# Two graph layers with nested Strassen-Winograd products: products in six steps, an order of its own for the first, second and last pair, and first transfers in a fixed order

## The chip, the cores and the metric

The kernel runs on one core of a Trainium2 chip. Its engines are TensorE (PE; PEld in the profile is its weight load), VectorE (DVE), ScalarE (ACT), GpSimd (POOL) and SyncE (SP), which here issues all DMA transfers. The metric is the time of one execution on the device in microseconds, lower being better. Products are accumulated in PSUM, which has eight banks of 512 fp32 columns per partition[...].

## The reference, cut to what matters

There are 64 graphs of 256 nodes with 512 features, all fp32. Two layers follow each other, each with a residual and a layer norm.

```python
def _L0_gnn_ref(x, adj, W):
    deg = jnp.sum(adj, axis=-1, keepdims=True)
    agg = jnp.einsum('bij,bjf->bif', adj, x) / jnp.maximum(deg, EPS)
    cat = jnp.concatenate([x, agg], axis=2)
    return jax.nn.relu(jnp.einsum('bnf,of->bno', cat, W))

def _L1_gnn_ref(X, adj, mask, Wqk, Wv):
    q, k = jnp.split(X @ Wqk, 2, axis=-1)
    v = X @ Wv
    agg = jnp.einsum('bij,bjd->bid', adj, k * mask[:, :, None])
    w = inv_scale * mask * jnp.einsum('bid,bid->bi', q, agg)
    return jax.nn.softmax(w, axis=1)[:, :, None] * v

x = _layernorm(x + _L0_gnn_ref(x, adj, L0_gnn_W), axis=-1)
x = _layernorm(x + _L1_gnn_ref(x, adj, nodemask, L1_gnn_Wqk, L1_gnn_Wv), axis=-1)
```

`x` is 64 x 256 x 512, `adj` 64 x 256 x 256, `W` 512 x 1024, `Wqk` 512 x 1024 and `Wv` 512 x 512.

## The kernel before

**Tiling.** Two graphs make a pair, so there are NP = 32 pairs. Nodes lie in two tiles of 128 (NT), features in four (NF). In layer 1 the two weight halves of Wqk are multiplied once, at the start, into one 512 x 512 matrix (`weight_product`, 16 matmuls of 512 columns from the tile `shared`), so that q·(adj k) becomes (x M)·(adj x).

**Products.** Each 512 x 512 by 512 product for a pair is cut by the Strassen-Winograd scheme into seven block products P1 to P7. Those named in `INNER` (P1, P2, P5, P3, P4) are cut a second time by the same scheme (`inner`): seven 256-column matmuls each, some into a scratch bank `w`, from which VectorE or ScalarE carry each partial result into the product's two banks `q`. The others (`outer`) are four plain 512-column matmuls. The sums of operand blocks are made by GpSimd (`inner_sums`, `fourth_sums`, `adj_sums`) and VectorE (`outer_sums`, `sums_T`). The adjacency product (`gather`) is one level of the same scheme.

**Units.** `inner` returns four closures: `first`, `second`, `third` and `last`, where `third` holds two matmuls and `last` two. `layer0` and `layer1` bind letters to the lists of closures: i, k, m, p, q, r, s are P1, P5, P2, P6, P7, P3, P4 of layer 0; J, N, K, H, Q, L, P are P1, P5, P2, P6, P7, P3, P4 of layer 1; a to g and A to G are the seven parts of the two gathers. `pw`, `pu`, `py` and `pf` are the four pairs of banks; the scratch bank of each product is passed by the caller.

**Order.** Nothing is issued directly. VectorE, ScalarE and GpSimd operations go through a `Recorder`, matmuls through `mm` and transfers through `send`, all into a `Plan`, with the bytes that they touch and an assumed duration. The string `ORDER` says in what sequence the letters' closures are called within a loop pass over pairs; the pass for pair j does layer 0 of pair j and layer 1 of pair j - 1. `when(...)` hangs further work on counts of letters done. TensorE's recorded sequence gives every step a due time; `Plan.order` then lists all engines' instructions, choosing by due time among the steps that its assumed durations say can start soon (within `SLACK`). The list so made is the program order of each engine, which runs its queue strictly in that order. After the loop the last pair's layer 1 is written out with `run(...)` calls.

**Lines that the steps below speak of.** L270 is the recorder's one line, so all VectorE, ScalarE and GpSimd work carries it; rows are told apart by their tiles. L355 is `mm`, L361 the transpose by TensorE, L790 the transpose of the last scores, L371 is `send`. Tiles: `own` is a pair's rows (result of layer 0, then x1, then the output); `xT`, `x1T` are the transposed inputs of the two layers, `_s` and `_i` their outer and inner sums; `t`, `t_i` are weight sums; `tv` the sums for the gathers; `fifth` a kept partial result; `less`, `var`, `rstd`, `shift` the columns of a layer norm (`norm_parts`): `less` is minus the mean, made by VectorE from `sum`; `row`, `top`, `total` and `probs` belong to `softmax`. There the scores of a pair, 128 x 4, are put into a 128 x 32 tile `wide`, turned, stored to `dram` and read back into all partitions as `row`, whose maximum `top` VectorE takes over 512 columns.

**Start.** Ten matmuls on a tile of ones come first. Transfers are sent in recorded order as far as due times allow; the built order begins with two `w` blocks, two `wqk` blocks, `xT`, two `wqk` blocks and two `w` blocks. `weight_sums` makes the sums of W0 and W1 on VectorE.

Of the kernel before, what the change touches and what calls it, by code (L numbers as in the profile page):

```python
# [16 lines left out]
P = 128  # L17
Q = 32
# [7 lines left out]
INNER = ("P1", "P2", "P5", "P3", "P4")  # L26
SLOTS_X = {"P1": 0, "P2": 1, "P5": 2, "P3": 2, "P6": 0, "P7": 1, "P4": 0}
SLOTS_X1 = {"P1": 0, "P2": 1, "P5": 2, "P6": 0, "P7": 1, **({"P3": 2, "P4": 0} if "P7" in INNER else {"P3": 0, "P4": 1})}
ORDER = ("L k k i i i L k k i m p p m p p q m q q q s r m s r r r a s b s d e J J c J J f K g K K K N H H "
         "N Q A D H H Q Q C E Q N G N P P B P P F L L")  # L30
# [32 lines left out]
class Plan:  # L63
# [78 lines left out]
    def latest(self):  # L142

        before, left, open_, n = defaultdict(list), {}, [], 0
        for s in self.steps:
            left[s] = len(s.next)
            for t, fresh in s.next:
                before[t].append((s, fresh))
# [72 lines left out]
def vec_cost(op, out, ins, more):  # L221
# [6 lines left out]
    if op in ("scalar_tensor_tensor", "tensor_scalar"):  # L228
        if n < 16:
            return 0.08, 0.158, both  # L230
        by_column = len(ins) > len(wide)
        return (n / 960 + (0.133 if by_column else 0.078),
                n / 960 + (0.21 if by_column else 0.15) + (0.08 if more else 0), both)
# [72 lines left out]
def resnorm_kernel(  # L306
# [58 lines left out]
    def send(out, in_):  # L365
        o, i = ap_of(out), ap_of(in_)
        n = columns_of(o) * o.ap[0][1] * 4
        issue, sent, done = (0.66, 0.66, 3.0) if n == 64 * 1024 else (0.41, n / 300000, 3.0)
        if i.ap[0][0] == 0:
            sent = 3.5  # L370
        plan.record("SP", lambda: nc.sync.dma_start(out, in_), [o], [i], issue, done, sent=sent)  # L371
# [32 lines left out]
    def load_xT(j, home=home_x):  # L404
        Xs[j] = Side(home, *sums_x, 0, SLOTS_X)
        for k in range(2):
            send(Xs[j].a[:, k].rearrange("p h e t n -> p (h e) (t n)"),
                 x_t[2 * j + k].rearrange("(c p) n -> p c n", p=P))
# [3 lines left out]
    for a in range(NA):  # L412
        send(wqk.rearrange("p (h a) f -> a p h f", h=2)[a],
             wqk_t.rearrange("(h a p) f -> a p h f", p=P, h=2)[a])
    w0_of = w_t.rearrange("(k h p) o -> k p h o", p=P, h=H)
    for k in (0, 2):
        send(w0[:, k * H:(k + 1) * H, :], w0_of[k])
    load_xT(0)
    for k in (3, 1):
        send(w0[:, k * H:(k + 1) * H, :], w0_of[k])  # L420
# [16 lines left out]
    drams = [dram.tile([P, Q], F32, name=f"dram{k}") for k in (0, 1)]  # L437
# [5 lines left out]
    def weight_sums(w, name):  # L443
        b11, b21, b12, b22 = (w[:, k * H:(k + 1) * H, :] for k in range(4))
        t1, t2, t4 = (mem.tile([P, H, F], F32, name=f"{name}{k}") for k in (1, 2, 4))
        it = mem.tile([P, 3, len(INNER), HF], F32, name=f"{name}i")
# [3 lines left out]
        def inner_of(p, b):  # L450
            if p not in INNER:
                return
            n = INNER.index(p)
            c11, c12, c21, c22 = (b[:, e, h * HF:(h + 1) * HF] for e in range(2) for h in range(2))
            i1, i2, i4 = (it[:, r, n] for r in range(3))
# [67 lines left out]
    def inner(p, X, sides, w, q, done=lambda: None, onto=None):  # L523
# [42 lines left out]
        def third():  # L566
# [5 lines left out]
            else:  # L572
                act.copy(q[1][:, :HF], lo)
                vec.tensor_add(q[1][:, HF:], lo, fifth[0])
            mm(q[0][:, :HF], X.chunk(block, 0, 1), b["B21"])

        def last():
            mm(q[1][:, :HF], X.chunk(block, 1, 1), b["T4"])
            mm(q[0][:, HF:], s(3), b["B22"])
            done()  # L580
        return [first, second, third, last]

    def product(p, X, sides, w, q, done, onto=None):
        if p in INNER:
# [88 lines left out]
    def norm_parts(src, total, n=NT):  # L673
        rstd, shift, less, var = (small(x, [P, n]) for x in ("rstd", "shift", "less", "var"))

        def squares():
            vec.tensor_scalar(less, total, -1.0 / F, None, op0=OP.mult)
# [70 lines left out]
    def softmax(j):  # L748
        w = wide[j % 2]
        scale_scores(j, w[:, :2 * NT].rearrange("p (k t) -> p k t", k=2))  # L750
        turned = small("turned", [P, Q], 2)
        vec.transpose(turned, w)
        d = drams[j % 2]
        send(d, turned)
        row = ring("row", [P, P // Q, 2 * NT * Q])
# [3 lines left out]
        rk = row.rearrange("p a (k c) -> p k a c", k=2)  # L759
        p = small("probs", [P, 2, NT], 2)  # L760
        vec.reduce_max(top, rk, axis=AX.XY, negate=True)
# [41 lines left out]
    def layer0(j, X, o, u, y):  # L803

        own, yt = owns[j], ys[j]
        make = lambda p, w, q, done, onto=None: product(p, X, W0, w, q, done, onto)
        return {
            "i": make("P1", pw[0], u, lambda k: act.copy(own[:, k, 0], u[k])),
            "k": make("P5", pw[1], y, lambda k: act.copy(yt[:, k, 1], y[k])),
            "m": make("P2", pw[0], o, lambda k: act.copy(own[:, k, 0], o[k]), own[:, :, 0]),  # L810
            "p": make("P6", pw[1], u, lambda k: vec.tensor_add(yt[:, k, 0], u[k], yt[:, k, 1])),
            "q": make("P7", pw[0], u, lambda k: vec.tensor_add(yt[:, k, 1], u[k], yt[:, k, 1])),
            "r": make("P3", pw[1], y, lambda k: act.copy(yt[:, k, 0], y[k]), yt[:, :, 0]),
            "s": make("P4", pw[0], u, lambda k: act.copy(own[:, k, 1], u[k])),
        }

    def layer1(j, Y, q, o, u, y, w1_, w2, w5, w3, w4, w6, w7):
# [3 lines left out]
        make = lambda p, w, q, done, onto=None: product(p, Y, W1, w, q, done, onto)  # L821
# [9 lines left out]
        def add_p5(k):  # L831
            vec.tensor_add(v[:, k], y[k][:, None, :].to_broadcast([P, NT, F]), v[:, k])
        return {
            "J": make("P1", w1_, u, lambda k: act.copy(q[:, k], u[k])),
            "K": make("P2", w2, o, lambda k: act.copy(q[:, k], o[k]), q),
            "H": make("P6", w6, u, lambda k: act.copy(v[:, k, 0], u[k])),
            "Q": make("P7", w7, u, lambda k: act.copy(v[:, k, 1], u[k])),
            "N": make("P5", w5, y, add_p5),
            "P": make("P4", w4, u, lambda k: dot(u[k], k, 1)),
            "L": make("P3", w3, y, lambda k: act.copy(v[:, k, 0], y[k]), v[:, :, 0]),  # L840
        }, dots

    def run(order, **units):
        for name in order.split():
            units[name].pop(0)()

# [14 lines left out]
    W0 = weight_sums(w0, "t0_")  # L861
# [6 lines left out]
    W1 = weight_sums(w1, "t1_")  # L868
# [5 lines left out]
    for j in range(NP):  # L874
# [4 lines left out]
        units, made = layer0(j, X, o, u, y), Counter()  # L879
        waiting = []  # L880

        def when(done, work):
            waiting.append((Counter(done), work))

        def start_gather0():
            units.update(gather("abcdefg", sumsA.pop(j), sums_T(ys[j]), pw[1], y[1], y[0],
                                own=own, rdeg=rdegs.pop(j)))

        def end_gather0():
            place = norm0(j)  # L890
            mask_adj(j)
            if place:
                when("PPPPL" if j else "", place)

        def x_sums(*ps):
            for p in ps:
                if p in INNER:
# [21 lines left out]
        when("kkkk", lambda: (fourth_sums(X), x_sums("P3")))  # L919
        when("iiii", lambda: x_sums("P6"))  # L920
        when("mmmm", lambda: x_sums("P7"))
        when("pppp" if "P6" in INNER else "iiii", lambda: x_sums("P4"))
        when("ppppqqqqrrrr", start_gather0)
        when("rrrrssss", next_x)
# [3 lines left out]
        else:  # L928
# [4 lines left out]
            new, dots = layer1(j - 1, Y, q_at, o2, u2, y2, pw[0], y[0], pw[1], pw[1], pw[0], pw[0], pw[1])  # L933
            made["L"] = 4 - len(ahead)
# [3 lines left out]
            def y_sums(*ps):  # L938
                for p in ps:
                    if p in INNER:  # L940
# [14 lines left out]
            def start_gather1():  # L955
                units.update(gather("ABCDEFG", sumsM.pop(j - 1), sums_T(owns[j - 1]), pw[0], o2[1], o2[0],
                                    aggs[j - 1]))
            when("LLLL" if j > 1 else "mmmm", start_layer1)
            when("JJJJ", lambda: y_sums("P6"))
            when("KKKK", lambda: y_sums("P7" if "P7" in INNER else "P4"))  # L960
            when("HHHH", lambda: (fourth_sums(Y), y_sums("P4" if "P7" in INNER else "P3")))
            if "P7" in INNER:
                when("HHHHNNNN", lambda: y_sums("P3"))
            when("gKKKK", start_gather1)
            when("BFKKKK", dots)
            when("ABCDEFG", next_adj)
        for name in ORDER.split():
            if name.isupper() and j == 0 or name == "L" and j == 1 and not made["J"]:
                continue
            units[name].pop(0)()  # L970
            made[name] += 1
# [109 lines left out]
```

## Time and profile before

| What | Value |
|---|---|
| Time, median of 3 runs | 1866.63 us (1865.25 to 1867.9) |
| Span of the profiled execution | 1865.2 us, 26366 instructions |
| TensorE clock granted, mean | 0.995 |
| One pair in the middle of the loop (two of 56.7 us, from 435.6) | PE 56.45, PEld 42.6, DVE 49.1, ACT 38.7, POOL 30.8 us busy |
| Front, 0 to 50 us | PE 45.95, DVE 34.7, POOL 24.0 us busy |
| 50 to 100 us | PE 46.6, DVE 45.8, ACT 28.4, POOL 36.1 us busy |
| 1800 us to the end | PE 48.6, DVE 46.3, ACT 43.2, POOL 17.6 us busy |
| `less<-sum`, VectorE, x126 | 138 ns shortest, 400 median, 722 longest; 50.6 us in all |
| `top<-row`, VectorE, x31 | 675 ns mean |

How to read it: a row of instructions gives start, duration, engine, line, operation, the tile written and those read, shapes, and how many in a row were merged ("x2"). The bracket at the end is the idle time of that engine before it and what ended the wait. An fp32 matmul is carried out in two passes, each with its own row, so "x2" is mostly one matmul of the program. The duration of a PE row is modelled and overlaps the next one; the distance of two starts is the real pace. An idle bracket counts from that modelled end, so it states less than what was lost against the pace.

### The profile page before, as it was taken

The page shows a single profiled execution, that of the slowest core. Times are in us where ns is not written, and L with a number is a line of the kernel's source. Part 1 is how long each engine was busy: PE and PEld are TensorE (multiplying, and loading weights), DVE is VectorE, ACT ScalarE, POOL GpSimd, SP SyncE. Part 2 cuts the span into 40 slices and gives each one's busy share as a digit, 9 for nine tenths or more (in the row PEclk, how much of TensorE's full clock was granted, in tenths as well). Part 3 has the DMA queues.
Part 4 walks back from the last instruction along what each step waited for, and adds up shares of the span by engine and source line. Part 5 has one row for each costly group of instructions (what it writes and reads, how often), then busy time and mean ns, then how long its engine had stood idle before and what let it go on. Part 6 is the DMA issues. An engine that isn't in the chain of part 4 may idle for free.

```text
span 1865.2 us, 26366 instructions
## 1 busy us (share of the span) xinstructions
PE 1834.0 (98%) x7382; PEld 1374.0 (74%) x7382; DVE 1595.6 (86%) x3511; ACT 1245.2 (67%) x3115; POOL 996.1 (53%) x1511
## 2 busy tenths in 40 slices
PE   9999999999999999999999999999999999999996
PEld 5777777777777777777777777777777777777774
DVE  6988988888888889888889888888888898888886
ACT  3656766667766668666667666677666686666665
POOL 4745555565545565545655555654456555456532
PEclk9999999999999999999999999999999999999998
DMA  7133333433333343233333333333333432343302
GB/s 238 46 78 99 101 82 97 109 107 95 103 87 96 97 116 93 81 103 108 97 102 99 84 97 108 108 94 98 91 98 97 115 92 79 106 109 97 98 11 74
DMA packets 380721, 181.35 MB, mean 97 GB/s; under 512 B 263712, under 2 KB 345248, under 8 KB 380576
## 3 DMA queue, kind: packets, MB, share of 16 engines
q1 hardware_dynamic: 380576, 179.67, 34.9%
q8 instruction: 60, 0.98, 0.2%
q14 instruction: 85, 0.70, 0.1%
HBM read 114.10 MB, written 34.06 MB: 79 GB/s over the span
## 4 chain that ended last, share of the span: by engine, by line
PE 83%; DVE 14%; issue 1%; ACT 1%; DMA 0%; SPq 0%; POOL 0%; ACTq 0%; DVEq 0%
PE bank L355 83%; DVE own L270 7%; DVE bank L270 3%; DVE less L270 1%; DVE y L270 1%; DVE x1T L270 1%; DMA shared<-wqk_t 0%; ACT junk L270 0%; DVE rdeg L270 0%; ACT own L270 0%; PE bank L361 0%; DVE turn L270 0%; DVE x L270 0%; DVE t_i L270 0%; ACT fifth L270 0%
## 5 line engine op out<-in xcount | busy, mean ns | idle before, releaser
L270 ACT COPY fifth<-bank 128x256 f32<-128x256 f32 x384 | 144.0, 376 | 302.0 <-PE bank L355 300.2
L270 POOL TENSOR_TENSOR x1T_i<-x1T 128x128 f32<-128x128 f32 (+1 forms) x128 | 81.0, 634 | 455.3 <-PE bank L355 315.8
L270 DVE TENSOR_TENSOR bank<-bank,fifth 128x256 f32<-128x256 f32 (+1 forms) x576 | 259.2, 456 | 44.1 <-PE bank L355 23.1
L270 ACT COPY shared<-bank 128x512 f32<-128x512 f32 x314 | 182.2, 582 | 66.1 <-PE bank L355 60.6
L355 PE MATMUL bank<-tv,sa 128*128 128x256 f32 x768 | 217.3, 379 | 0.2 <-DVE tv L270 0.2
L355 PE MATMUL bank<-w,x1T 128*128 128x512 f32 (+1 forms) x512 | 206.5, 486 | 0.0
L355 PEld LDWEIGHTS bank<-tv,sa 128*128 128x128 f32 x768 | 145.1, 190 | 81.9 <-issue 53.3
L270 ACT COPY bank<-bank 128x256 f32<-128x256 f32 (+1 forms) x352 | 145.4, 420 | 84.6 <-PE bank L355 74.2
L355 PE MATMUL bank<-w,xT 128*128 128x256 f32 (+1 forms) x496 | 200.0, 486 | 0.0
L270 ACT ACTIVATE junk<-own,less 128x512 bf16<-128x512 f32 x254 | 183.5, 723 | 21.0 <-DVE less L270 18.7
L270 DVE TENSOR_TENSOR y<-bank,y 128x512 f32<-128x512 f32 x192 | 132.2, 689 | 75.9 <-PE bank L355 72.1
L270 ACT ACTIVATE own<-own,shift,rstd 128x512 f32<-128x512 f32 x254 | 194.9, 824 | 2.8 <-DVE shift L270 2.6
L355 PE MATMUL bank<-t_i,x1T_i 128*128 128x256 f32 x640 | 187.3, 382 | 1.3 <-POOL x1T_i L270 0.7
L270 DVE TENSOR_TENSOR shared<-bank,shared 128x512 f32<-128x512 f32 (+1 forms) x157 | 137.6, 891 | 52.3 <-PE bank L355 52.0
L355 PE MATMUL bank<-t_i,xT_i 128*128 128x256 f32 x640 | 181.2, 379 | 0.0
L270 DVE SCALAR_TENSOR_TENSOR own<-bank,rdeg,own 128x256 f32<-128x256 f32 x384 | 174.8, 476 | 5.8 <-PE bank L355 1.9
L270 ACT COPY y<-bank 128x512 f32<-128x512 f32 x256 | 149.2, 585 | 45.1 <-PE bank L355 44.8
L355 PEld LDWEIGHTS bank<-t_i,xT_i 128*128 128x128 f32 x640 | 118.7, 190 | 72.0 <-issue 58.6
L355 PE MATMUL bank<-t,x1T_s 128*128 128x512 f32 (+1 forms) x384 | 168.2, 521 | 0.0
L355 PE MATMUL bank<-t,xT_s 128*128 128x512 f32 (+1 forms) x384 | 158.5, 521 | 0.1
L355 PEld LDWEIGHTS bank<-t_i,x1T_i 128*128 128x128 f32 x640 | 117.4, 189 | 28.1 <-issue 8.8
L270 ACT COPY own<-bank 128x512 f32<-128x512 f32 x192 | 112.5, 588 | 35.5 <-PE bank L355 35.1
(158 smaller groups left out, 4402.3 us busy)
## 6 DMA issues: line engine op xcount, KB each, us to landing
x<-x SPq DMA_DIRECT2D x64, 512.0 KB, 3.6
xT<-x_t SPq DMA_DIRECT2D x62, 512.0 KB, 3.8
out<-own SPq DMA_DIRECT2D x62, 512.0 KB, 3.8
x1T<-turn SPq DMA_DIRECT2D x480, 64.0 KB, 2.1
adj<-adj_t SPq DMA_DIRECT2D x64, 256.0 KB, 2.9
turn<-adj SPq DMA_DIRECT2D x64, 256.0 KB, 2.9
row<-dram SPq DMA_DIRECT2D x31, 256.0 KB, 5.3
w<-w_t SPq DMA_DIRECT2D x4, 512.0 KB, 7.4
```

The costliest lines, as they stand in the source:

```text
L270: self.plan.record(self.name, lambda: call(out, *args, **kwargs), outs, ins, busy, done, port)
L355: plan.record("PE", lambda: nc.tensor.matmul(ps, a, b, start=start, stop=True, skip_group_check=True), [ps], [a, b], busy, busy + 0.165, w ...
```

## The change

**Inner products in six steps.** `third` and `last` are split, so that each closure has one matmul (only `first` has two): first, second, third, fourth, last, closing. `INNER` becomes one tuple per layer, with the same members.

**Orders.** Four strings take the place of one string and the written-out `run` calls: `ORDER0` for pair 0, `ORDER1` for pair 1, `ORDER` for the others, and `ORDER9` for the last pair's layer 1, where `S` stands for scores, turns and exponentials and `Z` for the division. `when` takes the names of products (all their closures) instead of repeated letters.

**Scratch banks.** `HOME` and `HOME9` name for each letter one of the eight banks, counted through pu, py, pf, pw.

**First transfers.** `send` can take a due time; the nine first blocks get the fixed sequence wqk 0, w 0, w 2, wqk 1, xT, wqk 2, w 3, wqk 3, w 1.

**Work moved between engines.** W1's sums for P5, P3 and P4 go to GpSimd (12 operations of 256 columns); the weight sums `i` are three tiles instead of one. `less` is made by ScalarE. In `softmax`, VectorE takes the maximum of each of the 128 turned rows (32 columns) into a 33rd column before the store; `top` is then taken over 16 columns, and the exponential reads `row` without them.

**Planner.** No step is due later than 6 us after TensorE's recorded end, and `tensor_scalar` counts as using the port that VectorE shares with GpSimd.

```diff
+HOME = "i6 k7 m6 p5 q1 r7 s6 a7 b2 c3 J6 K2 H7 Q1 N7 L7 P6 A6 B4 C5"
+HOME9 = "J7 K7 H5 Q2 N6 L7 P1 A2 B3 C1"
-ORDER = ("L k k i i i L k k i m p p m p p q m q q q s r m s r r r a s b s d e J J c J J f K g K K K N H H "
-         "N Q A D H H Q Q C E Q N G N P P B P P F L L")
+ORDER0 = ("i k k i i i i k i k p k k p p p m r q r m m m q r q q s r r m s r s s a m b s s d e c f g")
+ORDER1 = ("k k i i i i i k k i m k p k p p p q m m r q m m q r q s s s m r r s r s r J a b s J J d J e J c "
+          "J f K H g K K K H Q K N K Q A H H N N D N C E Q Q N N G B L P P F P L L P P P")
+ORDER = ("i i i i k k k L k L L k i i p m m k m p q p q m p m r q m q s s s s r r s r J r a J J J b J d J "
+         "s e c J f K K g H K H K H K K N N H Q N A Q D Q C E Q N G P F B N N L L P P L P P P L")
+ORDER9 = ("A J J J D J C J J E K B H G H N Q N H K N N F K H Q N K Q Q N K K P P L P P L L P P S L L L Z")
...
+            s.due = min(s.due, self.clock + 6.0)
...
+    for n, (what, k) in enumerate(((load_wqk, 0), (load_w0, 0), (load_w0, 2), (load_wqk, 1), (first_xT, 0), (load_wqk, 2), (load_w0, 3), (load_wqk, 3), (load_w0, 1))):
+        what(k, n - 1000.0)
...
-        it = mem.tile([P, 3, len(INNER), HF], F32, name=f"{name}i")
+        it = [mem.tile([P, len(INNER[layer]), HF], F32, name=f"{name}i{r}") for r in (1, 2, 4)]
...
+            sub = gp.tensor_sub if p in by_gp else vec.tensor_sub
...
+
+        def fourth():
             mm(q[0][:, :HF], X.chunk(block, 0, 1), b["B21"])
 
         def last():
             mm(q[1][:, :HF], X.chunk(block, 1, 1), b["T4"])
+
+        def closing():
             mm(q[0][:, HF:], s(3), b["B22"])
             done()
-        return [first, second, third, last]
...
+        return [first, second, third, fourth, last, closing]
...
-            vec.tensor_scalar(less, total, -1.0 / F, None, op0=OP.mult)
+            act.activation(less, total, AF.Copy, scale=-1.0 / F)
...
-        turned = small("turned", [P, Q], 2)
-        vec.transpose(turned, w)
+        turned = small("turned", [P, Q + 1], 2)
+        vec.transpose(turned[:, :Q], w)
+        vec.reduce_max(turned[:, Q:], turned[:, :Q], axis=AX.X)
...
-        vec.reduce_max(top, rk, axis=AX.XY, negate=True)
+        vec.reduce_max(top, rk[:, :, :, :, Q], axis=AX.XY, negate=True)
+        rk = rk[:, :, :, :, :Q]
```

## The prediction

> **What bounds the kernel now.** I read the page first (busy shares, chain of waits), then the list of who waits for whom on PE, then the timeline in four places. Durations are of the profiled execution, span 1865.2 us; that run took 1867.0 us, and the runs shown go from 1865.25 to 1867.9.
>
> ```profile
> PE 1834.0 (98%) x7382; PEld 1374.0 (74%) x7382; DVE 1595.6 (86%) x3511; ACT 1245.2 (67%) x3115; POOL 996.1 (53%) x1511
> ...
> PE 83%; DVE 14%; issue 1%; ACT 1%; DMA 0%; SPq 0%; POOL 0%; ACTq 0%; DVEq 0%
> ...
> PE bank L355 <- DVE bank L270: 7.6, 30, 0.5
> PE bank L355 <- DMA shared<-wqk_t: 2.8, 1, 2.8
> ```
>
> TensorE is the bound and hardly idles; what it waits for repeatedly is VectorE writing into a PSUM bank, 30 times, once for each pair that uses ORDER. But a busy PE hides part of its loss, because the modelled end of a matmul runs past the start of the next. I therefore measure loss by starts. Each fp32 matmul appears as two passes; one of 256 columns takes 0.43 us from start to start (below, 603.31 to 603.74), one of 512 takes 0.86.
>
> ```profile
> 603.31 0.59 PE L355 MATMUL bank<-w,x1T_i 128*128 128x256 f32 x2
> ...
> 603.59 0.72 DVE L270 TENSOR_SCALAR less<-sum 128x2 f32<-128x2 f32 x1
> 603.74 0.59 PE L355 MATMUL bank<-tv,adj 128*128 128x256 f32 x2
> ...
> 604.23 0.47 DVE L270 SCALAR_TENSOR_TENSOR own<-bank,rdeg,own 128x256 f32<-128x256 f32 x1
> ...
> 604.61 0.59 PE L355 MATMUL bank<-own,adj 128*128 128x256 f32 x2
> 604.62 0.68 DVE L270 TENSOR_TENSOR bank<-bank,y 128x512 f32<-128x512 f32 x1
> ...
> 605.45 0.67 PE L355 MATMUL bank<-t_i,x1T 128*128 128x256 f32 x2 [0.25 <-DVE bank L270]
> ...
> 605.96 0.38 PE L355 MATMUL bank<-t_i,x1T_i 128*128 128x256 f32 x1
> ```
>
> This is the steady loss. From 604.61 to 605.45 are 0.84 us for 0.43 us of work, and from 605.45 to 605.96 another 0.08 too many: 0.49 us. A further 0.10 us occurs once per pair at a `t_i,xT_s` product (in the pass starts). A pair takes 56.7 us, so 0.59 us is 1%; 30 pairs make 17.7 us.
>
> ```profile
> 4.63 0.42 DVE L270 TENSOR_TENSOR t_i<-w 128x256 f32<-128x256 f32 x1 [3.54 <-DMA w<-w_t]
> 7.74 6.63 PE L355 MATMUL bank<-shared 128*128 128x512 f32 x11 [2.79 <-DMA shared<-wqk_t]
> 10.46 0.34 PEld L355 LDWEIGHTS bank<-shared 128*128 128x128 f32 x1 [0.52 <-issue]
> 11.20 0.19 PEld L355 LDWEIGHTS bank<-shared 128*128 128x128 f32 x1 [0.40 <-issue]
> ...
> 88.28 0.70 PE L355 MATMUL bank<-t_i,x1T_i 128*128 128x256 f32 x2 [0.61 <-DVE t_i L270]
> 89.56 1.13 PE L355 MATMUL bank<-tv,adj 128*128 128x256 f32 x4 [0.57 <-DVE tv L270]
> 92.45 1.13 PE L355 MATMUL bank<-own,adj 128*128 128x256 f32 x4 [0.86 <-ACT bank L270]
> 94.69 0.70 PE L355 MATMUL bank<-t_i,x1T_i 128*128 128x256 f32 x2 [0.68 <-POOL x1T_i L270]
> ...
> 1849.58 1.05 PE L355 MATMUL bank<-total,fifth 1*128 1x1 f32 x8 [0.68 <-DVE total L270]
> 1849.84 0.72 ACT L270 ACTIVATE junk<-own,less 128x512 bf16<-128x512 f32 x1 [0.28 <-DVE less L270]
> ```
>
> The front: the first transfer (a `w`) has landed at 4.63, the warm-up matmuls on `ones` end at 4.99, but the first real matmul starts at 7.74, and its passes then come 0.85 us apart instead of 0.43 until 11.2. Lost: 2.75 + 1.75 = 4.5 us. The first two pairs: starts against the pace give 0.8, 0.8, 1.1 and 0.8 us at the four places shown, and with the small ones between 15 and 200 us 7.5 us in all. The end: PE's last matmul is over at 1850.6; ScalarE then normalises the last but one pair's rows (begun at 1849.84) ahead of the last pair's, and 14.6 us pass to the end.
>
> **What the Trainium skill says.** "TensorE: Matmul & The Clock Gate", Part 1: TensorE runs at half clock until about 3.4 us of activity and falls back when idle. The trace agrees: the 512-column passes at 7.74 to 11.2 take double. "SBUF — State Buffer", section "SBUF: two separate sides": VectorE and GpSimd share a port pair, locked for a whole instruction. The trace agrees: `less`, 256 numbers, takes 0.14 us at the tail and 0.72 at 603.59, beside a GpSimd add of 0.73 us begun at 603.56. "Perfetto Trace Analysis", section "Optimization Strategy": the same gap repeating on the saturated engine can mean too little PSUM for the next tile. Here the repeated gap is indeed a PSUM bank's half, but VectorE's queue is what makes it late.
>
> **The change, part by part.** Both programs hold 3726 PE instructions of equal kinds and 876 on SP, so the work of the bound engine is unchanged; only losses can move.
>
> (1) The loop. The matmul that stalls (`t_i,x1T`, last unit of K) needs a 512-wide VectorE addition that follows K's third product (the `w,x1T_i` at 603.31). By the built programs' order three 256-column matmuls lay between the two: 1.29 us. In the changed program five do, one of 512 columns: 4 x 0.43 + 0.86 = 2.57 us. Before, the addition began 0.9 us after its product had drained (603.31 + 0.43 + about 0.17 = 603.9, to 604.62), because `less` held VectorE until 604.31. Now `less` goes to ScalarE, and VectorE's `top` over 512 columns (675 ns mean, once per pair) becomes a maximum over 32 columns before the store and one over 16 after it; I estimate these at 0.15 us each, from the small VectorE rows of 0.14 to 0.17. VectorE sheds 2 x 0.40 + 0.38 = 1.2 us of its 49 per pair. Against it: in the new VectorE queue five instructions stand between the preceding `bank<-bank,y` and this addition: 3 x 0.43 to 0.47 of `own<-bank`, a `tv` of 0.68, a 512-wide `own` of about 0.83, 2.9 us; with both additions 4.0 us, plus some 0.2 of handover. PE works 6 x 0.43 + 2 x 0.86 = 4.3 us over the same stretch. It fits, barely. I book 0.37 of the 0.59, x 30 = 11 us. Bounds: 0 (the wait stays or moves) to 17.7 us.
> ScalarE gets two more `less` per pair (estimate 0.2 us each, from `rstd` at 0.20): 0.4 us on 38.7 of 56.7, hidden. Behind it on that queue stand `junk` and bank copies; the copies feed PE, so one may come 0.2 us later. The tightest copies in both orders have two matmuls (0.86 us) between, less the copy's 0.37 and about 0.2 of handover: 0.29 us of room (VectorE's additions at such places: 0.86 - 0.43 - 0.2 = 0.23). They did not stall before; it holds unless two things meet. HOME names for the inner products of the loop the same banks as before (6, 7 and 2); outer products don't use theirs. So "from all eight" acts only in the last pair. Zero. The 33rd column makes the row transfer 3% larger and it lands 5.3 us after issue, unhurried: zero.
>
> (2) The front. Landings before were at 4.63, about 6.1 and 7.74, and the ninth at 16.07: 1.43 us per 512 KB. The new order puts `wqk` blocks at places 1, 4, 7 and 9: 4.63, 8.9, 13.2, 16.1. PE: 4.99 + 4 x 0.86 = 8.4, waits 0.5; to 12.3, waits 0.9; to 16.6, no wait. Losses 1.4 for 4.5, and gaps below 1 us leave the clock up. Booked 2.8; bounds 0 (PE then waits for `xT` sums) to 3.2.
>
> (3) First two pairs. Twelve 256-column subtractions of W1's sums (418 ns median, up to 946) leave VectorE, some 5 us out of the jam at 80 to 95, for GpSimd at about 0.72 us, 8.6 us in all, placed between its sums for pairs 0 and 1, before pair 0's second layer asks. GpSimd was 72% busy from 50 to 100 us: room 14 us. In the old order three waiting matmuls had less PE work ahead than their copy or add needs by itself (short by up to 0.36 us); in the new one none has. Booked 5 of 7.5; bounds -2 to 7.
>
> (4) The end. In the new queues the rows of the last but one pair are dotted, squared and mostly scaled before or during the last products (three scales of 0.73 remain after the exponentials). After PE's end remain on ScalarE about 2.2 (scales, overlapped), two squares of 0.9, four short steps of 0.25, two scales of 0.8, and VectorE's last 0.7: some 7.7 us, plus 3.4 from the last VectorE end (1861.8) to the span's end now: 11.1 instead of 14.6. Against it: only three matmuls (1.3 us) now cover the chain from P4's last product to `w`, with a 1.2 us add of `x` ahead of `w` on VectorE: I charge 1.5. Net 2; bounds -1.5 to 4.
>
> Sum: 11 + 2.8 + 5 + 2 = 20.8 us off the span; taken from the median of the three runs, 1866.6 - 20.8 = 1846.
>
> **Rivals.**
> A (chance 0.54): as summed, own range 1839 to 1851.
> B (0.27): the loop's wait mostly stays or moves to one of the places with 0.23 to 0.29 us of room, costing 0.3 us per pair more than booked: 9 us come back, 1855. For it: the 4.2 us in 4.3 above. Against: VectorE is lighter, and the port that stretched `less` is asked for less often.
> C (0.08): nothing moves in the loop, the 0.59 stays, for instance because x1T's transfers or GpSimd release that matmul and not VectorE: 1866.6 - 9.8 = 1857. Against it: the addition ends at 605.30, just ahead of the stalled start.
> D (0.05): new waits of 0.7 us per pair eat all: 1866, no change.
> E (0.06): slower. ScalarE, with `less` ahead of `junk` and 62 `row` activations in finer pieces, gives scratch banks back late at two of the tight places of a pair; each costs 0.41 + 0.10 as the present stall does. 30 x 1.02 = 31 us against 20.8: 1877. It decides beyond 0.8 us of new waits per pair. Against: ScalarE has 18 us free per pair.
>
> **How the numbers follow.** The likeliest is A, 1846. The range reaches down to nearly the best of all four parts (17.7 + 3.2 + 7 + 4 = 31.9 gives 1835; I stop at 1838, all four at once being unlikely) and up past B and C to 1859; D, E and the lower scrap are left out, 0.15 or so. Within 0.2% means within 3.7 us, about what this kernel's measurement can tell. A, B and C are faster: 0.89; D 0.05; E 0.06.
>
> **What would show it.** The line "PE <- DVE bank" loses its 30 waits; starts around `t_i,x1T` follow at 0.43 us; a pair takes 56.2 to 56.4 us. The first `shared` matmul starts near 5.0 with 0.43 us passes. Between 80 and 95 us no PE wait over 0.4. PE's end to span end is near 11 us. Wrong if a new releaser appears 30 times, above all ACT `fifth` or `bank`, if POOL `x1T_i` waits grow between 50 and 100 us, or if the end's wait for `w` exceeds 2.5 us.

## The result and the profile after

The changed kernel takes 1852.43 us (median of 4, 1851.55 to 1854.15) against 1866.65 us before (1865.25 to 1867.9): ratio 0.9925, 95% interval 0.9908 to 0.9942. That is 14.2 us faster; forecast were 20.8. The profiled execution has a span of 1849.8 us (its run took 1851.55).

The string `ORDER` of the changed kernel differs from the one in the diff above in three places (an `r` more, a `J` and an `L` less); the one that ran is

```python
ORDER = ("i i i i k k k L k L L k i i p m m k m p q p q m p r m r q m q s s s s r r s r J r a J J J b J d "
         "s e c J f K K g H K H K H K K N N H Q N A Q D Q C E Q N G P F B N N L P P L P P P L")
```

The page of the changed kernel (busy shares, then the chain of waits by engine and by line), with its list of PE's waits (us in total, times, longest):

```profile
PE 1830.3 (99%) x7382; PEld 1383.7 (75%) x7382; DVE 1541.1 (83%) x3402; ACT 1266.1 (68%) x3243; POOL 1025.5 (55%) x1523
...
PE 92%; DMA 3%; DVE 2%; SPq 2%; ACT 1%; issue 1%; POOL 0%; ACTq 0%; DVEq 0%
PE bank L364 92%; DMA turn<-adj 2%; SPq L380 2%; DVE y L279 1%; DMA xT<-x_t 0%; POOL xT_i L279 0%; ACT turn L279 0%; DVE bank L279 0%; DVE own L279 0%; ACT fifth L279 0%; DVE turn L279 0%; PE bank L370 0%; DVE x L279 0%; ACT own L279 0%; ACT junk L279 0%
...
PE bank L364 <- ACT fifth L279: 4.5, 9, 1.2
PE bank L812 <- DVE w L279: 2.0, 1, 2.0
...
PE bank L364 <- DMA shared<-wqk_t: 1.0, 2, 0.6
PE bank L364 <- DVE bank L279: 0.5, 1, 0.5
```

VectorE has shed 54 us, and its 30 waits are down to one. In their place stand nine waits for ScalarE's `fifth`, which is a kept partial result copied out of a scratch bank. The chain says where that comes from: it now passes through `turn<-adj`, a transfer of adjacency rows, and through SyncE's queue.

The waits understate the loss, so I again use the starts of matmul passes. In the traces the median pass of 256 columns takes 0.216 us from start to start and one of 512 columns 0.429. I count against 0.2135 and 0.427, some 2 ns less, and sum what the distances exceed this by over a stretch; differences between kernels hardly depend on this choice. The last column is the time from the start of PE's last matmul to the span's end. The losses in a row are from one profiled execution; the kernels from e1 on are described further on.

| Kernel | us, median | to 15 us | 15 to 200 | 200 to 1750 | 1750 to PE's last | after it |
|---|---|---|---|---|---|---|
| before | 1866.65 | 4.2 | 9.1 | 32.2 | 5.7 | 14.9 |
| changed | 1852.43 | 1.3 | 3.3 | 30.6 | 5.5 | 10.0 |
| booked gain | 20.8 | 2.8 | 5 | 11 | end: 2 | |
| e1, rows awaited later | 1842.35 | 1.9 | 3.5 | 20.9 | 5.5 | 10.0 |
| e2, rows awaited earlier | 1874.59 | 1.3 | 6.4 | 47.7 | 9.0 | 10.2 |
| e3, before, `less` on ScalarE, replanned | 1873.77 | 2.5 | 11.8 | 32.9 | 5.3 | 17.1 |
| e4, old loop order, replanned | 1871.81 | 1.1 | 5.7 | 46.0 | 8.1 | 10.0 |
| f1, before, `less` on ScalarE, same queues | 1854.54 | 2.4 | 9.4 | 20.0 | 5.3 | 14.9 |
| f2, e1 with `less` on VectorE | 1851.02 | 1.0 | 3.6 | 29.2 | 5.8 | 10.1 |
| f3, e1 with W1's sums on VectorE | 1843.08 | 1.4 | 4.0 | 20.8 | 8.4 | 10.2 |
| f4, e1 with the old last pair | 1847.24 | 0.9 | 3.4 | 21.1 | 7.6 | 13.2 |
| g1, changed, row transfers left out | 1842.58 | 1.4 | 3.2 | 21.5 | 5.5 | 10.2 |
| g2, e1 with old first pairs | 1857.13 | 1.3 | 10.6 | 26.8 | 6.0 | 10.0 |
| g3, e1 without the cap | 1846.99 | 1.9 | 3.3 | 21.4 | 6.2 | 13.5 |
| g4, before, new first transfers | 1864.82 | 2.0 | 9.3 | 32.0 | 5.7 | 15.0 |

Front, first pairs and end together give 2.9 + 5.8 + 0.2 + 4.9 = 13.8 us; the loop gives only 1.6. These make 15.4, the difference of the two spans. So the question is where the loop's 11 us went.

Some 14 us of each kernel's loop column are shares of under 40 ns per pass, common to all: the 2 ns by which the usual pass exceeds what I count against. The rest, before, is 27 times the stall of K's last unit (0.41 + 0.08 + 0.05 us) and 26 times 0.11 us at `t_i,xT_s`. In the changed kernel both are gone. Fourteen pairs have a new one at `w,xT_i -> t,xT`, of 0.16 to 1.32 us (7.2 us in all, and 1.7 in the pass after it), and every pair has three small pauses of 0.08 (6.6 us). Here is one of the new stalls, in the timeline of the changed kernel, SyncE's, ScalarE's and TensorE's rows:

```profile
402.37 0.56 SPq L380 DMA_DIRECT2D dram<-turned  x1
403.03 0.90 SPq L380 DMA_DIRECT2D turn<-adj  x2
...
406.59 0.42 ACT L279 ACTIVATE turn<-turn 128x256 f32<-128x256 f32 x1 [8.45 <-DMA turn<-adj]
...
407.01 0.40 ACT L279 ACTIVATE turn<-turn 128x256 f32<-128x256 f32 x1
...
407.40 0.35 ACT L279 COPY fifth<-bank 128x256 f32<-128x256 f32 x1
...
406.38 0.59 PE L364 MATMUL bank<-w,xT_i 128*128 128x256 f32 x2
407.81 0.70 PE L364 MATMUL bank<-t,xT 128*128 128x256 f32 x2 [0.83 <-ACT fifth L279]
```

The matmul at 407.81 should have started at 406.81, 0.43 us after the one before it. It writes into the scratch bank that `fifth` copies, and the copy waits in ScalarE's queue behind two activations that sum adjacency rows (`degrees`). Those wait for rows that SyncE issued at 403.03, 3.6 us earlier. The same place before the change, ScalarE's rows of the timeline:

```profile
528.68 0.37 ACT L270 COPY fifth<-bank 128x256 f32<-128x256 f32 x1 [8.88 <-PE bank L355]
528.95 0.42 ACT L270 ACTIVATE turn<-turn 128x256 f32<-128x256 f32 x1
```

There the copy stands first and waits for TensorE alone. The groups of the changed kernel (count, busy and mean ns, then idle before them) show how regular this is, and what `less` costs on ScalarE:

```profile
L279 ACT ACTIVATE turn<-turn 128x256 f32<-128x256 f32 x128 | 52.2, 410 | 216.7 <-DMA turn<-adj 216.6
...
L279 ACT ACTIVATE less<-sum 128x2 f32<-128x2 f32 x126 | 25.9, 205 | 9.0 <-DVE own L279 9.0
```

In 30 pairs ScalarE waits some 7 us for the rows. Most of it costs nothing, because no product needs a copy in that time; only what exceeds it does. The trace bears this out pair by pair: waits of up to 7.44 us are followed by no stall, and each of the 14 longer ones by a stall of its excess over some 7.46 us (a wait of 7.83 by one of 0.37, of 8.45 by 1.00, of 8.78 by 1.32). From the page, these transfers landed 2.9 us after issue before the change and 3.8 after it; the planner assumes 3.0.

The front and the end of the changed kernel, in its timeline:

```profile
4.92 3.70 PE L364 MATMUL bank<-shared 128*128 128x512 f32 x8
...
9.01 3.70 PE L364 MATMUL bank<-shared 128*128 128x512 f32 x8 [0.39 <-DMA shared<-wqk_t]
...
1835.11 0.60 PE L812 MATMUL bank<-ident,w 128*1 128x128 f32 x4 [2.04 <-DVE w L279]
...
1837.28 2.21 ACT L279 ACTIVATE own<-own,shift,rstd 128x512 f32<-128x512 f32 x3
...
1840.30 0.72 ACT L279 ACTIVATE junk<-own,less 128x512 bf16<-128x512 f32 x1
```

The first real product starts with the end of the warm-up at full pace. At the end, ScalarE has scaled the last but one pair's rows by 1839.5, before the last pair's rows need it at 1840.3.

### The profile page after: what moved, and what is told of

The parts are those of the page before. It is cut to its first block, busy times and chain, and to the rows that moved or that the text cites. A ratio compares the mean times of both kernels' runs of the same rounds, so it can differ in the third digit from the quotient of the medians.

```text
span 1849.8 us, 26279 instructions
## 1 busy us (share of the span) xinstructions
PE 1830.3 (99%) x7382; PEld 1383.7 (75%) x7382; DVE 1541.1 (83%) x3402; ACT 1266.1 (68%) x3243; POOL 1025.5 (55%) x1523
## 4 chain that ended last, share of the span: by engine, by line
PE 92%; DMA 3%; DVE 2%; SPq 2%; ACT 1%; issue 1%; POOL 0%; ACTq 0%; DVEq 0%
PE bank L364 92%; DMA turn<-adj 2%; SPq L380 2%; DVE y L279 1%; DMA xT<-x_t 0%; POOL xT_i L279 0%; ACT turn L279 0%; DVE bank L279 0%; DVE own L279 0%; ACT fifth L279 0%; DVE turn L279 0%; PE bank L370 0%; DVE x L279 0%; ACT own L279 0%; ACT junk L279 0%
## 5 line engine op out<-in xcount | busy, mean ns | idle before, releaser
L279 POOL TENSOR_TENSOR x1T_i<-x1T 128x128 f32<-128x128 f32 (+1 forms) x128 | 76.0, 604 | 488.7 <-PE bank L364 380.5
L279 DVE TENSOR_TENSOR bank<-bank,fifth 128x256 f32<-128x256 f32 (+1 forms) x576 | 251.7, 457 | 80.3 <-PE bank L364 44.1
L364 PE MATMUL bank<-tv,sa 128*128 128x256 f32 x768 | 212.4, 379 | 0.0
L279 ACT ACTIVATE turn<-turn 128x256 f32<-128x256 f32 x128 | 52.2, 410 | 216.7 <-DMA turn<-adj 216.6
L364 PE MATMUL bank<-w,xT 128*128 128x256 f32 (+1 forms) x496 | 195.7, 486 | 0.0
L364 PE MATMUL bank<-t_i,x1T_i 128*128 128x256 f32 x640 | 194.9, 387 | 0.1
L364 PE MATMUL bank<-t_i,xT_i 128*128 128x256 f32 x640 | 190.0, 380 | 0.2 <-POOL xT_i L279 0.2
L279 DVE SCALAR_TENSOR_TENSOR own<-bank,rdeg,own 128x256 f32<-128x256 f32 x384 | 172.7, 478 | 13.3 <-PE bank L364 12.4
L279 ACT COPY y<-bank 128x512 f32<-128x512 f32 x256 | 143.3, 584 | 55.7 <-PE bank L364 50.7
L364 PE MATMUL bank<-t,xT_s 128*128 128x512 f32 (+1 forms) x384 | 163.5, 522 | 0.0
L364 PEld LDWEIGHTS bank<-t_i,xT_i 128*128 128x128 f32 x640 | 118.9, 190 | 48.2 <-issue 20.9
```

What stands on the lines that cost most here:

```text
L279: self.plan.record(self.name, lambda: call(out, *args, **kwargs), outs, ins, busy, done, port)
L364: plan.record("PE", lambda: nc.tensor.matmul(ps, a, b, start=start, stop=True, skip_group_check=True), [ps], [a, b], busy, busy + 0.165, w ...
```

## The experiments

Theory R: ScalarE, waiting for the adjacency rows at the head of its queue, holds back the `fifth` copy and so gives back what the loop had gained. The rivals are theory V (VectorE's tight queue, the reason of the prediction's case B) and theory S (the small pauses). For the stall of before, theory P (`less` on VectorE beside GpSimd) stands against theory O (the distance in the order).

**e1: the planner is told a later landing.**

```diff
+        if o.tensor.name.startswith("turn") and n != 64 * 1024:
+            done = 4.5
```

> The changed kernel, in which the planner is told that the two transfers of adjacency rows into the tile turn land 4.5 us after their start instead of 3.0. In the order that it then writes, TensorE's and VectorE's queues stay as they are in the loop; ScalarE copies the first scratch half (fifth) of the layer's first product before, not after, the first two activations on these rows. Theory R (ScalarE stands waiting for the rows, with the fifth copy that TensorE needs queued behind): the stalls at w,xT_i -> t,xT, 7.2 us in 14 pairs of the changed kernel, go, and the time falls by 5 to 8 us, to 1844 to 1847. Theory V (VectorE's queue, 4.2 us of work in a stretch of 4.3, makes those matmuls late): its queue is the same, so the stalls stay and the time is 1852 within 1.5 us. Theory S (the 0.08 us pauses are what eats the gain, and the large stalls are mere consequences of an earlier delay): under 2 us gained.

Measured: 1842.35 us (1841.7 to 1844.71), ratio to before 0.987 (0.9855 to 0.9885), 10.1 us less than the changed kernel, more than the 5 to 8 expected. The loop lost 20.9 us instead of 30.6. The timeline of e1 at the same pair:

```profile
405.66 0.37 ACT L279 COPY fifth<-bank 128x256 f32<-128x256 f32 x1 [7.58 <-PE bank L364]
406.47 0.42 ACT L279 ACTIVATE turn<-turn 128x256 f32<-128x256 f32 x1 [0.44 <-DMA turn<-adj]
...
406.32 0.59 PE L364 MATMUL bank<-w,xT_i 128*128 128x256 f32 x2
406.75 0.59 PE L364 MATMUL bank<-t,xT 128*128 128x256 f32 x2
```

The rows still land 3.5 us after issue, but the copy is ahead of them, and `t,xT` follows at 0.43 us. All 14 stalls are gone; the pauses of 0.08 are all still there (6.5 us). R holds, V and S fall. One assumed duration, changed by 1.5 us, is worth more than two thirds of the whole change, and this kernel beats both others.

**e2: an earlier landing.** The same lines with 2.0 instead of 4.5.

> The same edit the other way: a landing of 2.0 us is assumed, and ScalarE has all four activations on the rows ahead of that fifth copy. Theory R: the copy comes another two activations, 0.65 us, later; the 14 stalled pairs lose 0.65 us more each and the others, which had up to 0.65 us of room, up to as much: 9 to 16 us more than the changed kernel, 1861 to 1868, and PE's waits for ACT fifth show it. Theory V and theory S: no more than 2 us of difference.

Measured: 1874.59 us, 22 more than the changed kernel, slower than before the change (ratio 1.0039, 1.0027 to 1.0052). The list of PE's waits in e2:

```profile
PE bank L364 <- ACT fifth L279: 19.2, 24, 1.5
```

The sign is R's, the size above its range: by starts, 27 pairs now stall at this place, 0.87 us on average against 7.2 us in 14 pairs; besides, some 3 us more each were lost in the first pairs and at the end (there by a fall of TensorE's pace, see the last section). I had taken the other pairs to have most of 0.65 us of room; they had little.

**g1: the wait itself taken away.** Every queue of the changed kernel in its order, without the loop's row transfers.

```diff
             send(rows[j][:, k], adj[2 * j + k].rearrange("(t p) j -> p t j", p=P))
+            if j > 1:
+                plan.steps[-1].issue = None
...
-            self.tc.keep_in_program_order(s.issue())
+            if s.issue is not None:
+                self.tc.keep_in_program_order(s.issue())
```

> The changed kernel with every queue in its order, but the transfers of adjacency rows into turn left out for the pairs from the third on (60 of 64): the degrees are then those of whatever lies in the tile, a part of the computation that is left out. Theory R (ScalarE stands waiting for these transfers): its activations come up to 4 us earlier, the fifth copy behind them with them, the stalls at w,xT_i -> t,xT go, and the time is 1841 to 1845. If it is the place of the copies and of the mask activations in ScalarE's queue (which e1 moved too) and not the wait: the stalls stay, 1851 to 1854.

Measured: 1842.58 us (1842.46 to 1845.22), as in e1. In its timeline the activations keep their place ahead of the copy, but wait for the transfers that empty the tile, some 4.5 us before the copy is wanted:

```profile
400.41 0.42 ACT L280 ACTIVATE turn<-turn 128x256 f32<-128x256 f32 x1 [3.06 <-DMA x1T<-turn]
...
404.94 0.37 ACT L280 COPY fifth<-bank 128x256 f32<-128x256 f32 x1 [3.62 <-PE bank L365]
```

With the queue unchanged and only the transfers gone, the loss goes: it is the wait, not the position.

**e3 and e4: one part undone or done, with the planner at work again.** e3 is the kernel before with the line of `less` exchanged as in the diff above; e4 is the changed kernel with the loop's old `ORDER` in six-step letters (and one `L` fewer in `ORDER1`, since two products' steps are carried over differently).

```diff
-            vec.tensor_scalar(less, total, -1.0 / F, None, op0=OP.mult)
+            act.activation(less, total, AF.Copy, scale=-1.0 / F)
```

> The kernel before with one edit: the scaled row sums (less) are computed on ScalarE instead of VectorE; everything else, the orders of the pairs included, is as before, though the planner writes its queues anew. Theory P (the prediction's: less, stretched to 0.7 us while GpSimd holds the port, makes the addition late that TensorE waits for at own,adj -> t_i,x1T): that stall of 0.41 us falls to under 0.1 us in all 27 pairs, 11 us or so, 1854 to 1857 unless new waits come. Theory O (only the greater distance in the new order removes it, since VectorE's queue between product and addition is long in any case): the stall stays at 0.2 us or more, 1862 to 1867.

> The changed kernel with the loop's old order of products (its four steps written as the six new ones, so that the sequence of products is that of the kernel before) and all other parts as changed. Theory P: less being off VectorE, the old stall at own,adj -> t_i,x1T does not come back, and the loop loses no more than in the changed kernel: 1845 to 1853. Theory O: the stall comes back at 0.4 us a pair, and the time is 1856 to 1862. In this kernel the first fifth copy stands ahead of ScalarE's activations on the rows, so theory R expects no stall at w,xT_i -> t,xT or its like there.

Measured: 1873.77 and 1871.81 us, both slower than before. The stall `own,adj -> t_i,x1T` is absent in e3 and left in three pairs of e4, much as P says, but neither P nor O foresaw what came. In e3 thirteen pairs stall by 0.62 us elsewhere, which the list of PE's waits puts down to a ScalarE copy:

```profile
PE bank L355 <- ACT shared L270: 5.9, 13, 0.5
```

In e4 fifteen waits for VectorE's `bank` (4.7 us) and many small ones are spread over changing places. The edit changed not one instruction but the whole list: in e3 4063 of TensorE's 7382 rows and 617 of GpSimd's 1511 are others than stood at their place before, in e4 5180 and 815 of 1523 are others than in the changed kernel, since the planner decides anew from the first difference on. The times of these two runs say nothing on the parts they were meant for.

**f1 and f2: `less` moved with the queues held.** The planner lists as usual; only the issue of that step is exchanged, so that all other instructions keep their order. f1 does it to the kernel before, f2 undoes it in e1.

```diff
+            n0 = len(plan.steps)
             vec.tensor_scalar(less, total, -1.0 / F, None, op0=OP.mult)
+            plan.steps[n0].issue = lambda: nc.scalar.activation(less, total, AF.Copy, scale=-1.0 / F)
```

> The kernel before with all its queues kept in their order, but the instruction less issued on ScalarE at the place in the list where it stood for VectorE. Theory P (less, stretched to 0.7 us beside GpSimd, is what makes the addition late): the stall of 0.41 us at own,adj -> t_i,x1T goes in all 27 pairs, with the 0.08 and 0.10 after it perhaps: 9 to 14 us off, 1853 to 1858. Theory O (distance in the order): it stays above 0.2 us, 1861 to 1867. If ScalarE's copies come late by less ahead of them, new waits for ACT appear and the time is 1862 or more with the old stall gone.

> The kernel of e1 (the changed kernel with the rows' landing assumed at 4.5 us; 1842.4 us), all queues kept in their order, but less issued on VectorE again. Theory P: VectorE's 4.2 us in a stretch of 4.3 no longer fit once less takes up to 0.7 us: waits for DVE bank or DVE own of 0.2 to 0.5 us come in each pair, 6 to 14 us more, 1848 to 1857. Theory O: with 2.57 us of products between, the addition is in time in spite of less: 1842 within 1.5 us.

Measured: f1 1854.54 us (ratio to before 0.9929, 0.9917 to 0.9942), f2 1851.02, 8.7 more than e1. The timeline of f1 where before had its stall:

```profile
598.35 0.59 PE L355 MATMUL bank<-w,x1T_i 128*128 128x256 f32 x2
...
598.63 0.48 DVE L270 SCALAR_TENSOR_TENSOR own<-bank,rdeg,own 128x256 f32<-128x256 f32 x1
...
599.03 0.69 DVE L270 TENSOR_TENSOR bank<-bank,y 128x512 f32<-128x512 f32 x1
599.03 0.21 ACT L679 ACTIVATE less<-sum 128x2 f32<-128x2 f32 x1
...
599.64 0.59 PE L355 MATMUL bank<-own,adj 128*128 128x256 f32 x2
600.08 0.59 PE L355 MATMUL bank<-t_i,x1T 128*128 128x256 f32 x2
```

The addition begins 0.68 us after its product's start instead of 1.31, and `t_i,x1T` follows at 0.44 us. The loop's loss falls from 32.2 to 20.0 us. In f2 it rises from 20.9 to 29.2, at another place: 28 times 0.20 + 0.11 us at `t,x1T_s -> tv,sa`, ahead of which `less` again takes 0.60 us. The timeline of f2:

```profile
482.14 0.73 POOL L279 TENSOR_TENSOR x1T_s<-x1T,x1T_s 128x256 f32<-128x256 f32 x1
482.28 0.60 DVE L701 TENSOR_SCALAR less<-sum 128x2 f32<-128x2 f32 x1
...
484.49 0.59 PE L364 MATMUL bank<-t,x1T_s 128*128 128x256 f32 x2
...
485.11 1.13 PE L364 MATMUL bank<-tv,sa 128*128 128x256 f32 x4
```

So P holds in both orders: `less` on VectorE costs the loop 12.2 us in the old and 8.3 in the new one. O is right in one point: the old stall itself does not come back in f2, where the addition stands ahead of `less`. With `less` on ScalarE, the new order brings nothing further (20.9 in e1 against 20.0 in f1), and f1's time is about that of the whole change.

No run tried P's reason, the GpSimd operation beside `less`, by itself, but the trace of before leaves little doubt. Of the 126 `less`, 89 took more than 0.25 us; every one of them began while a GpSimd operation ran, and ended 0.02 to 0.03 us after it. The other 37 met none. The partner of the `less` at 603.59 that the prediction shows, which ended at 604.31:

```profile
603.56 0.73 POOL L270 TENSOR_TENSOR x1T_s<-x1T,x1T_s 128x256 f32<-128x256 f32 x1 [0.77 <-PE bank L355]
```

**f3 and g2: the first pairs.** f3 issues W1's twelve subtractions on VectorE again, queues held (as in f1); g2 gives e1 the old order in the first two pairs, in six-step letters.

```diff
+                if eng is gp:
+                    plan.steps[-1].issue = lambda: nc.vector.tensor_sub(to, c, d)
```

> The kernel of e1, queues in their order, but the twelve subtractions for W1's sums issued on VectorE at the places where they stood for GpSimd. If they are what the jam at 80 to 95 us was made of: TensorE's loss between 15 and 200 us, 3.5 us in e1, returns by 2 to 5 us, 1844 to 1848. If the first pairs' own orders did it: 1842 within 1.5 us.

> The kernel of e1 with the old order of products in the first two pairs (four steps written as six). If their own orders took out the jam, as the run with W1's sums back on VectorE suggests: TensorE's loss between 15 and 200 us returns from 3.5 to 8 us or more, 1846 to 1849. If W1's sums on GpSimd and the order each do for it: within 1.5 us of 1842.

Measured: f3 1843.08 us (1842.4 to 1845.49), no difference from e1; the loss from 15 to 200 us is 4.0 against 3.5. g2 1857.13: that loss is 10.6, and the jam is back at its old place (between 75 and 100 us 6.1 us are lost, 4.2 before the change, 0.4 in e1 and f3). So the orders had removed it, wherever W1's sums are made. Its longest wait in g2 is for a weight sum that VectorE still makes:

```profile
PE bank L363 <- DVE t_i L278: 1.9, 1, 1.9
```

But g2 overshot its range, because the planner also wrote the loop differently (26.8 against 20.9). Only the 7.1 us before 200 us can be the first pairs' share, and even these hold some 1.8 us of slower pace (see the last section) and what replanning did there; e3, with the old orders and one operation moved, lost 11.8.

**f4 and g3: the end.** f4 gives e1 the old last pair (order and scratch banks); g3 takes only the cap on the due times out.

```diff
-HOME9 = "J7 K7 H5 Q2 N6 L7 P1 A2 B3 C1"
+HOME9 = "J7 K6 H7 Q7 N7 L6 P7 A2 B3 C1"
+ORDER9 = ("A B C D J E J G J J F J J K K K K H H K K H H N N N N Q Q Q Q N N P P L P P L P P L L S L L Z")
```

> The kernel of e1 with the last pair's old order and banks (its four steps written as six). If the last pair's own order is what shortened the end: PE's wait for w falls from 2.0 back to 0.7 us and the stretch from PE's end to the span's end grows from 9.6 back to 13 to 15 us: 1844 to 1847. If the cap on the due times did it (which lets the last but one pair's rows be normalised earlier): the stretch stays at 10 us or less and the time is 1841 to 1843.

```diff
-            s.due = min(s.due, self.clock + 6.0)
```

> The kernel of e1 without the cap on the due times. The last pair's own order gave 4.9 us. If the cap has a share of its own in the shorter end: the stretch from PE's end to the span's end grows by 1.5 us or more and the time is 1844 to 1846. If not: 1842 within 1 us. Loop and front as in e1 in both.

Measured: 1847.24 and 1846.99 us, 4.9 and 4.6 more than e1. The ScalarE rows of the timeline, first f4 (PE's last start 1832.2), then g3 (1831.8):

```profile
1834.75 0.70 ACT L279 ACTIVATE junk<-own,less 128x512 bf16<-128x512 f32 x1
...
1836.43 0.80 ACT L279 ACTIVATE own<-own,shift,rstd 128x512 f32<-128x512 f32 x1
1837.23 1.50 ACT L279 ACTIVATE own<-own,shift,rstd 128x512 f32<-128x512 f32 x2
```

```profile
1833.93 2.93 ACT L278 ACTIVATE own<-own,shift,rstd 128x512 f32<-128x512 f32 x4
1836.77 0.70 ACT L278 ACTIVATE junk<-own,less 128x512 bf16<-128x512 f32 x1
```

In f4 three of the four scales of the last but one pair stand behind the last pair's squares and run on to 1838.7; in g3 all four stand ahead of those squares, as before the change. In e1 they are over by 1830.4, beside the last products. From PE's end to the span's end it is 12.8 us in f4 and 13.1 in g3, against 9.6 in e1. So each has a share, with both times a little above the ranges expected, and the gain is not the sum of two: either one missing loses nearly all of it. (PE's wait for `w`, expected to fall in f4, grew to 2.7 us.)

**g4: the first transfers alone**, in the kernel before, queues held.

```diff
+    first = plan.steps[-10:]
+    plan.first = [first[n] for n in (0, 4, 5, 1, 6, 7, 2, 8, 3, 9)]
```

> The kernel before with all queues in their order, only the ten first transfers issued in the changed kernel's order. The prediction's step 2: the first shared matmul starts near 5.0 us at full pace, the loss up to 15 us falls from 4.2 by 2.8, and the time is 1863.5 to 1865. Rival: the products of the first pair then wait for xT's or w's sums instead, which lay hidden behind the late start, and the time is 1866 to 1868.

Measured: 1864.82 us, ratio 0.9986 (0.9979 to 0.9992), so 2.4 us; the loss to 15 us falls by 2.1. There is one wait for `wqk`, of 2.1 us, where the changed kernel has two of 0.4 and 0.6; with the same transfers, the remainder comes with its new queues. Before the change the wait there was 2.8 us, so only 0.7 of the 2.1 is waiting saved; the rest is the half pace that followed that wait and is absent in g4.

## Why the prediction was right and wrong

The direction and the range held; 1846 was 6.4 us too low. That it came so near is in part luck: the loop fell 9.4 us short, and the end gave 3.1 more than booked, beyond its upper bound of 4.

**Step 1, the loop: 11 booked, 1.6 obtained.** The removed stall was read rightly: with `less` gone from VectorE the addition is in time. What its removal is worth came out in size too: 11.3 us between before and e1. But the prediction left 0.22 of the 0.59 us per pair standing without naming what would keep it; in e1 all 0.59 go and the three new pauses bring 6.5 us, which nobody foresaw, so the agreement is partly luck. A pair takes 56.26 us in e1, as forecast, and 56.3 to 57.7 in the changed kernel. What failed is the sentence that ScalarE's load is "hidden" and its copies hold "unless two things meet". I priced ScalarE's queue by its busy time, 18 us free per pair, and by the room between product and copy. I did not look in the new queue for instructions that wait on a transfer, and for what stands behind them. The Trainium skill, "Perfetto Trace Analysis", section "Tensor Engine Instruction (MATMUL, LD_WEIGHTS)", says that ScalarE's queue, unlike TensorE's, is strictly first in, first out; the timeline at 406.59 agrees, an idle ScalarE with a copy behind. The copy had been moved behind the first two activations on the rows, and 9.7 us came back (30.6 less 20.9). That is case B in form and almost in price (9 us), but not at the places it named and not through VectorE. Case E had the right engine with too high a price; e3 shows that such a thing does happen there. The greater distance in the order, to which I gave half of the argument, was not needed once `less` was gone (f1); with `less` back on VectorE the new queue has the addition ahead of it, and the loop loses 3.0 us less than before (29.2 in f2 against 32.2).

**Step 2, the front: 2.8 booked, 2.9 obtained**, with the waits near 9.0 and 13.3 at 0.4 and 0.65 us where 0.5 and 0.9 were computed. (4.5 less the 1.4 computed would be 3.1; 2.8 was booked without a reason for the 0.3.) The 1.75 us of half pace in it are less certain than they look: f1 and e3, with the old order of transfers, did not have them in their profiled executions. The medians of g4 and before, over 21 and 25 runs, give 2.4.

**Step 3, the first pairs: 5 booked, 5.8 obtained, for a wrong reason.** W1's sums on GpSimd, the reason priced, are worth 0.5 us of loss (f3). The orders were the cause (g2: up to 7.1 us), as the side remark said. Its reason, three matmuls with too little work ahead of their copy or add, is not shown; g2's longest wait there was for a weight sum.

**Step 4, the end: 2 booked, 5.1 obtained.** The stretch after PE shrank by 4.9 instead of 3.5, since the last scales of the last but one pair were over (at 1839.5) before PE's end (1840.2), where 2.2 us of them were counted after it. (The parts listed for what remains add to 7.3 us, not 7.7, which makes the 3.5 into 3.9.) The 1.5 us charged for PE's longer wait for `w` were right for that wait (0.7 to 2.0) but not for the stretch, whose other losses fell by as much (5.7 to 5.5).

**The parts booked at zero.** `less` takes 0.205 us on ScalarE, as estimated. The finer row maxima take 0.19 and 0.18 us instead of 0.15 each; they and the scratch banks alone were not tried.

**Open.** What lengthens the rows' landing from 2.9 to 3.8 us, and what lets SyncE's sixteen `x1T` transfers, ahead of the rows in its queue, take 10.0 us in one pair and 11.5 in another: 12 of the 14 stalls follow one of 10.4 us or more, the other two a landing above 4.1. And what makes the three pauses of 0.08 us per pair.

## What to carry to other kernels

On an engine with an in-order queue, ask of every new queue which instruction waits for a transfer and what stands behind it; busy shares don't show it, but a row such as "216.6 us idle <- DMA" ahead of a cheap group does. Where a planner writes the queues from assumed durations, the assumed landing of a DMA is part of the kernel: compare it with the measured one. And to find out what one part of a change does, hold the order of everything else fixed; letting the planner run again replaces the experiment by another kernel.

## What the runs showed of the hardware

After PE waits of 2 to 3 us the pace sometimes fell to half. Before the change it did so at the start, after 2.8 us; in f1 and e3, with 2.1 and 2.2 us at that place, it did not, so 1.8 us of what f1 gains on before in the first column is not its edit's doing. In f3 and e2, after 2.3 and 2.0 us for `w`, the pace held for 0.4 to 0.9 us and then fell until PE's end: passes that take 0.32 and 0.31 us in e1 took 0.59 and 0.56. In f4, after 2.7 us, the next passes of 256 columns took 0.43 us instead of 0.216, and 3.2 us after the wait the full pace was back; in g2, after 1.9 us, seven in a row took 0.43 to 0.59. In the changed kernel, e1 and g1, waits of 2.0 us for `w` were followed by full pace. The Trainium skill, "TensorE: Matmul & The Clock Gate", Part 1, puts the fall at an idle time of about 3.4 us. These waits were all shorter, so here the measurement goes beyond the page; each is from one execution, and what else decides is not shown. The timeline of f3:

```profile
1826.19 0.60 PE L817 MATMUL bank<-ident,w 128*1 128x128 f32 x4 [2.27 <-DVE w L279]
...
1828.58 1.22 PE L364 MATMUL bank<-w,x1T_i 128*128 128x256 f32 x2 [0.53 <-DVE total L279]
...
1832.34 1.22 PE L364 MATMUL bank<-t_i,x1T_s 128*128 128x256 f32 x2
```

A moved instruction of 256 numbers was worth nearly as much as the whole change: on VectorE it lasted 0.40 us on average before the change (0.30 in f2), on ScalarE 0.21, and moving it was worth 12.5 us (1867.04 to 1854.54, runs side by side); 126 of them made 50.6 us of VectorE's busy time.
